# Turning normalized rows: 32x32 blocks on the DVE and a trip through memory in place of TensorE transposes

## The chip, the core and the metric

The kernel runs on one core of a Trainium2 chip. The metric is device time in microseconds (us) of one execution. The engines are TensorE (PE, with its weight loads as PEld), VectorE (DVE), ScalarE (ACT), GpSimd (POOL) and SyncE (SP). SP does no arithmetic here: it issues DMAs. POOL issues DMAs too, those that convert or accumulate.

## The reference

Two layers of masked attention over 16 batches of 1024 tokens with 256 features, in float32. Layer 0 has four heads of 64, layer 1 eight heads of 32.

```python
# for each of two layers (weights and number of heads differ; layer 1 has biases for q, k and v)
h = jnp.maximum(_layernorm(x, axis=-1), 0.0)          # normalized rows, then relu
q, k, v = h @ Wq, h @ Wk, h @ Wv                      # split into heads
scores = q @ k.T / sqrt(D)
scores = where(adj > 0, scores, -inf)                 # adj: 1024 x 1024 a batch
out = softmax(scores, axis=-1) @ v
x = x + concat(heads of out) @ Wo.T + bo
```

x is (16, 1024, 256), adj is (16, 1024, 1024) of int32, about 3% ones.

## The kernel before

**Layout.** A batch is worked in two halves of 512 tokens. The rows of x of one half lie in a tile [128, 4, 256]: token 128 t + p is at partition p, slot t. Scores are computed transposed, keys on partitions and 512 queries along the row, so q and k are needed as [features, tokens]. That is what the turn is for: the normalized rows `hn` (tokens on partitions) become `hT` (features on partitions).

**Inputs of a half.** `stats` (DVE statistics, then four small POOL instructions), `norm` (four ACT instructions into `hn`, one buffer), `add_bias` (a POOL DMA that adds bo to x), `turn` (eight PE transposes into a PSUM pair, L209, and one ACT copy to `hT`, L210, two buffers), then `k`, `q` and `values`, matrix products from `hT` of about 3.7 us of PE each.

**Steps.** A layer's attention is cut into groups (a half of the queries times half of the heads), and a group into steps. Layer 0 has 16 steps a batch, layer 1 has 32. In a step PE computes four score blocks (L400) into two PSUM pairs; for each pair DVE applies the mask (L416) and ACT the exponential (L422); two steps later PE multiplies the result p by v (L434). The score blocks share three PSUM pairs with every other product. The sums of p for the softmax are formed by adding tiles of p: on DVE and POOL (L443 to L449) in layer 0; in layer 1 on POOL (L535) and by DMAs that add one tile of p into another (`accumulate`, L521, 1 MB each). PE then adds over partitions (L301, `pz`).

**End of a group.** `copy_out` (ACT, L312) brings the product to `cat`. `spread` copies the sums from PSUM to `s` (ACT, L320) and spreads them by DMA over the partitions (L333); `invert` takes the reciprocal (DVE, L341), writes it to memory as `vd` (L343) and reads it back over the partitions of each head as `inv` (L346); `normalize` multiplies on POOL (L352). After two groups `end_half` multiplies by Wo (L381), adds to x (L386) and, after layer 1, stores it.

**Masks.** For each of eight tiles of a batch's adj: `load` (POOL DMA with conversion to bf16 into `adj`, one buffer, L131), `flip` (SP's DMA transpose into `adjT`, one buffer, L137), `put` (ACT, L146, into the mask as fp8), and later `second` (ACT, L154).

**Order.** The order is written out by hand. `stream.later(i, f, ...)` puts function f into step i; within a step, small work comes first, then `turn` and the products. Each engine and each DMA-issuing queue runs its instructions in the order in which they were recorded, and a wait holds back all that stands behind it on the same queue. The batch loop interleaves layer 0 of batch b+1 (steps `a` to `a + 15`) with layer 1 of batch b (steps `c` to `c + 31`); `mine` is layer 1 of batch b, `other` is layer 0 of batch b+2. One pass of this loop is 48 steps. The lines that place the turns of a pass after the first, `half_inputs(inp, half, turn, k, q, values)`:

```python
half_inputs(mine, 0, a - 13, a, a + 2, a + 8)        # a - 13 is c + 19 of the pass before
half_inputs(mine, 1, a - 1, c, c + 6, c + 2)         # a - 1 is c + 31 of the pass before
half_inputs(other, 0, c + 1, c + 8, c + 16, c + 18)
half_inputs(other, 1, c + 9, c + 22, c + 26, c + 30)
```

Of the kernel before, what the change touches and what calls it, by code (L numbers as in the profile page):

```python
# [10 lines left out]
F32 = mybir.dt.float32  # L11
# [3 lines left out]
AF = mybir.ActivationFunctionType  # L15
# [3 lines left out]
P = 128  # L19
# [66 lines left out]
def fast_program(ctx, tc, a, w, loads, chk):  # L86
# [3 lines left out]
    nc = tc.nc  # L90
    x, adj, out = a["x"], a["adj"], a["out"]
    B, N, E = x.shape
# [5 lines left out]
    actp = ctx.enter_context(tc.tile_pool(name="actp", bufs=2))  # L98
# [14 lines left out]

    xs = {}

    def open_x(b, half):
        t = xp.tile([P, 4, E], F32, tag=f"x{half}", name=f"x_{b}_{half}")
        nc.sync.dma_start(t, x[b, ts(half, 512), :].rearrange("(t p) e -> p t e", p=P))
        xs[b, half] = t


# [35 lines left out]
    class Inputs:  # L157
# [25 lines left out]
                self.shift[half] = small.tile([P, 4], F32, tag="shift", bufs=3, name=f"shift_{n}")  # L183
                nc.gpsimd.tensor_mul(self.shift[half], less, self.rstd[half])

        def norm(self, half, tiles=range(4)):
            n = f"{self.n}_{half}"
            if 0 in tiles:
                self.hn[half] = work.tile([P, 4, E], F32, tag="hn", bufs=1, name=f"hn_{n}")
            for i in tiles:  # L190
                nc.scalar.activation(
                    self.hn[half][:, i, :], xs[self.b, half][:, i, :], AF.Relu,
                    bias=self.shift[half][:, i : i + 1], scale=self.rstd[half][:, i : i + 1],
                )

        def add_bias(self, half):
# [3 lines left out]
                rows, w.bo[self.layer].unsqueeze(1).to_broadcast([P, 4, E]), accum_op=ALU.add  # L200
            )

        def turn(self, half):
            hn = self.hn.pop(half)
            self.hT[half] = actp.tile([P, 2, 512], F32, tag="hT", name=f"hT_{self.n}_{half}")
            pt = psum_pair(f"ph_{self.n}_{half}")
            for c in range(2):
                for i in range(4):
                    nc.tensor.transpose(pt[:, c, ts(i, P)], hn[:, i, ts(c, P)], w.ident)  # L209
            nc.scalar.copy(self.hT[half], pt)  # L210

        def kq(self, half, is_q):
            if half == 0 and not is_q:
# [58 lines left out]
    class Group:  # L272
# [36 lines left out]
        def copy_out(self):  # L309
            if self.g == 0:  # L310
                self.half.cat = work.tile([P, 2, 512], F32, tag="cat", name=f"cat_{self.n}")
            nc.scalar.copy(self.half.cat[:, self.g, :], self.o)  # L312

        def lanes(self, t):
            return t.rearrange("r (c f) -> (r c) f", f=self.n_f)
# [1 line left out]
        def spread(self):  # L317

            s = work.tile([P, 512], F32, tag="s", bufs=1, name=f"s_{self.n}")
            nc.scalar.copy(s, self.s)  # L320
            inp, k = self.inp, 2 * self.qh + self.g
            if k == 0:

                pool, tag = small, f"sums{self.layer}"
                if self.layer and inp.b == B - 1:
                    pool, tag = adjp, "adj"
                inp.sums = pool.tile(
                    [P, 4 * self.n_f], F32, tag=tag, bufs=1, name=f"sums_{inp.n}"
                )
            self.sn = inp.sums[:, ts(k, self.n_f)]  # L330
            lanes = P // self.per
            for r in range(self.per):
                nc.sync.dma_start(  # L333
                    self.sn[r * lanes : (r + 1) * lanes, :],
                    s[r * self.D : r * self.D + 1, :].rearrange("r (c f) -> r c f", f=self.n_f),
                )
# [17 lines left out]
        def finish(self):  # L354

            inp, qh = self.inp, self.qh
            inv = work.tile([P, 512], F32, tag="inv", bufs=1, name=f"inv_{self.n}")
            py = psum_pair(f"py_{self.n}").rearrange("p a (t e) -> p (a t) e", e=E)
            rows, cat = xs[inp.b, qh], self.half.cat
            dst = out[inp.b, ts(qh, 512), :].rearrange("(t p) e -> p t e", p=P)  # L360
            for h in range(2):
                q = ts(h, 256)
                nc.vector.reciprocal(inv[:, q], self.s[:, q])
                nc.vector.tensor_mul(cat[:, self.g, q], cat[:, self.g, q], inv[:, q])
                for i in (2 * h, 2 * h + 1):
                    for c in range(2):
                        nc.tensor.matmul(
                            py[:, i, :], cat[:, c, ts(i, P)], w.o[self.layer][:, c, :],
                            start=(c == 0), stop=(c == 1),
                        )  # L370
            for h in range(2):
                t = ts(h, 2)
                nc.vector.tensor_add(rows[:, t, :], py[:, t, :], rows[:, t, :])
                nc.sync.dma_start(dst[:, t, :], rows[:, t, :])

        def end_half(self):
            inp, qh = self.inp, self.qh
            py = psum_pair(f"py_{self.n}").rearrange("p a (t e) -> p (a t) e", e=E)
            for i in range(4):
                for c in range(2):  # L380
                    nc.tensor.matmul(  # L381
                        py[:, i, :], self.half.cat[:, c, ts(i, P)], w.o[self.layer][:, c, :],
                        start=(c == 0), stop=(c == 1),
                    )
            rows = xs[inp.b, qh]
            nc.vector.tensor_add(rows, py, rows)  # L386
            if self.layer:
                nc.sync.dma_start(
                    out[inp.b, ts(qh, 512), :].rearrange("(t p) e -> p t e", p=P), rows
                )  # L390

    def scores(st):
        gr = st.gr
# [66 lines left out]
    class Stream:  # L460
# [12 lines left out]
        def later(self, i, f, *args):  # L473
            self.due.setdefault(i, []).append((f, args))
# [116 lines left out]
    mask, inp = masks[0], inputs[0][0]  # L591
# [11 lines left out]
    inp.stats(0)  # L603
    load(0)
    load(1)
    inp.norm(0)
    inp.stats(1)
    load(2)
    load(3)
# [7 lines left out]
    flip(1)  # L617
    open_w(1)
    inp.k(0)
    inp.norm(1)  # L620
    for u in range(4, NT):
        load(u)
    inp.q(0)
# [41 lines left out]
    stream = Stream(steps)  # L665
    later = stream.later

    def norms(inp, half, *at):

        for i, f in zip(at, (inp.stats, inp.stats, inp.norm, inp.norm)):  # L670
            later(i, f, half, (0, 1) if i in (at[0], at[2]) else (2, 3))
        later(at[3] + 1, inp.add_bias, half)

    def half_inputs(inp, half, *at):

        for i, f in zip(at, (inp.turn, inp.k, inp.q, inp.values)):
            later(i, f, half)


# [6 lines left out]
        later(i - 2, masks[1].flip, t)  # L686
        later(i, masks[1].put, t)
    later(9, bias_of_v)
    norms(inputs[0][1], 0, 2, 3, 5, 6)
    half_inputs(inputs[0][1], 0, 7, 8, 10, 12)  # L690
    norms(inputs[0][1], 1, 6, 7, 9, 10)
    half_inputs(inputs[0][1], 1, 13, 14, 20, 16)
    for b in range(B - 1):
        mine, a, c = inputs[1][b], first[b + 1], second[b]
        if b == 0:

            norms(mine, 0, a + 5, a + 6, a + 8, a + 9)
            half_inputs(mine, 0, a + 11, a + 12, a + 14, a + 14)
            norms(mine, 1, a + 13, a + 14, a + 15, c)
            half_inputs(mine, 1, c + 1, c + 3, c + 6, c + 4)  # L700
        else:
            norms(mine, 0, a - 20, a - 19, a - 16, a - 15)
            half_inputs(mine, 0, a - 13, a, a + 2, a + 8)
            norms(mine, 1, a - 14, a - 10, a - 8, a - 6)
            half_inputs(mine, 1, a - 1, c, c + 6, c + 2)
        for i, u in zip((0, 2, 4, 6, 8, 10, 12, 13), range(NT)):
            later(a + i, masks[b].second, u)
        if b + 2 < B:
            other, mask = inputs[0][b + 2], masks[b + 2]
            later(a + 5, open_x, b + 2, 0)  # L710
            later(a + 13, open_x, b + 2, 1)
            if b == 0:
                norms(other, 0, a + 14, a + 15, c + 2, c + 3)
                half_inputs(other, 0, c + 5, c + 8, c + 16, c + 18)
                norms(other, 1, c + 3, c + 4, c + 6, c + 7)
                half_inputs(other, 1, c + 11, c + 22, c + 26, c + 30)
            else:
                norms(other, 0, a + 10, a + 12, a + 13, a + 15)
                half_inputs(other, 0, c + 1, c + 8, c + 16, c + 18)
                norms(other, 1, c, c + 4, c + 5, c + 6)  # L720
                half_inputs(other, 1, c + 9, c + 22, c + 26, c + 30)
            for i, t in zip((7, 12, 17, 22, 33, 37, 41, 45), range(NT)):
                later(a + i - 6, mask.load, t)
                later(a + i - 3, mask.flip, t)
                later(a + i, mask.put, t)
        else:
            last, e = inputs[1][b + 1], c + 32
            norms(last, 0, c + 5, c + 6, c + 8, c + 9)
            half_inputs(last, 0, c + 11, c + 14, c + 16, c + 20)
            norms(last, 1, c + 13, c + 14, c + 16, c + 17)  # L730
            half_inputs(last, 1, c + 19, c + 24, e + 6, e + 4)
            for u in range(NT):
                later(c + 8 + 2 * u, masks[b + 1].second, u)
    stream.run()
# [249 lines left out]
```

## Time and profile before

| | |
|---|---|
| median of 3 runs | 3334.15 us (3329.18 to 3335.32) |
| the profiled execution's own time | 3336.89 us |
| its span, first to last instruction | 3335.1 us |
| mean granted TensorE clock | 0.991 |
| one pass of the batch loop, from the accumulates that recur in the chain | about 205 us |
| the turn: 512 transposes (L209), 64 copies (L210) | 72.0 us of PE, 64.2 us of ACT |
| PE waiting for `hT`, before values, k or Wo | 16.2 + 2.5 + 1.9 us |
| POOL's mask load waiting for a flip | 76.4 us, 29 times |
| DMA, moved | 361.08 MB, mean 108 GB/s |

The page gives, for each engine, the time in which it was busy and its share of the span; busy PE time has modelled ends. The chain of work that ended last is followed back from the last instruction, at each step to what released it; what stands in it set the end. A timeline lists one engine's instructions by start, with its idle time before them and who ended it. In the view by stretches the figures after the engines are the clock, the busy share of the 16 DMA engines and GB/s.

### The profile page before, as it was taken

How to read it: one execution, taken by the hardware profiler on the slowest of the kernel's cores; microseconds unless marked ns; L12 is line 12 of the kernel's file. 1: busy time of each engine (PE TensorE's matmuls, PEld its weight loads, DVE VectorE, ACT ScalarE, POOL GpSimd, SP SyncE). 2: the span in 40 equal slices, each digit the busy share in tenths (PEclk: the TensorE clock that was granted, in tenths of full speed). 3: DMA queues.
4: the chain of work that ended last, by engine and by line, in shares of the span. 5: the costliest groups of instructions: out<-in, count | busy, mean ns of one | idle time of the engine just before them, and what ended most of it. 6: DMA issues, size and time to landing. Idle time of an engine off the chain costs nothing.

```text
span 3335.1 us, 44057 instructions
## 1 busy us (share of the span) xinstructions
PE 3245.4 (97%) x16766; PEld 1272.1 (38%) x16766; DVE 2391.8 (72%) x2600; ACT 2308.4 (69%) x2530; POOL 2349.9 (70%) x1274
## 2 busy tenths in 40 slices
PE   8999999999999999999999999999999999999998
PEld 3443333433434343343434334333333433333333
DVE  5677776777767677676777767767677776776766
ACT  5667676776767767677676766767767676676765
POOL 4568576785867858677686766867768576685776
PEclk9999999999999999999999999999999999999999
DMA  7338467384663836548375583755737557383441
GB/s 147 66 66 150 93 111 140 75 154 87 123 125 80 160 82 130 112 94 148 79 141 101 99 140 77 136 106 106 135 80 146 105 105 138 71 146 78 85 85 31
DMA packets 313485, 361.08 MB, mean 108 GB/s; under 512 B 190001, under 2 KB 257841, under 8 KB 290481
## 3 DMA queue, kind: packets, MB, share of 16 engines
q0 software_dynamic: 77856, 253.78, 42.3%
q1 hardware_dynamic: 235408, 104.41, 13.9%
q8 instruction: 133, 2.18, 0.3%
q14 instruction: 88, 0.71, 0.1%
HBM read 119.54 MB, written 17.56 MB: 41 GB/s over the span
## 4 chain that ended last, share of the span: by engine, by line
PE 72%; POOL 8%; DMA 8%; DVE 4%; ACT 4%; issue 3%; SPq 1%; POOLq 0%; DVEq 0%; ACTq 0%
PE ps L400 24%; PE po L434 21%; PE pq L226 11%; PE pv L262 6%; POOL p L535 5%; PE py L381 5%; DMA p<-p 4%; PE pz L301 3%; DVE p L416 3%; DMA adjT<-adj 2%; ACT p L422 2%; PE ph L209 1%; POOL p L446 1%; ACT mask L146 1%; DMA vd<-vn 1%
## 5 line engine op out<-in xcount | busy, mean ns | idle before, releaser
L416 DVE SCALAR_TENSOR_TENSOR p<-mask,ps 128x1024 f32<-128x1024 fp8e5 x1536 | 1793.8, 1215 | 698.8 <-PE ps L400 606.5
L422 ACT ACTIVATE p<-p 128x1024 f32<-128x1024 f32 x1536 | 1614.5, 1057 | 820.5 <-DVE p L416 776.1
L535 POOL TENSOR_TENSOR p<-p,p 128x2048 f32<-128x2048 f32 x255 | 1202.5, 4718 | 171.0 <-PE po L434 157.7
L400 PE MATMUL ps<-qT,kT 32*128 32x512 f32 (+1 forms) x6144 | 1194.0, 638 | 25.6 <-DVE p L416 23.9
L434 PE MATMUL po<-p,v 128*32 128x512 f32 (+1 forms) x6144 | 998.1, 606 | 1.8 <-ACT cat L312 1.8
L400 PEld LDWEIGHTS ps<-qT,kT 32*128 32x128 f32 (+1 forms) x6144 | 383.0, 185 | 724.8 <-issue 374.5
L447 POOL TENSOR_TENSOR p<-p 128x1024 f32<-128x1024 f32 x128 | 301.8, 2358 | 298.3 <-DVE p L446 293.2
L434 PEld LDWEIGHTS po<-p,v 128*32 128x32 f32 (+1 forms) x6144 | 229.2, 118 | 696.6 <-issue 509.8
L446 POOL TENSOR_TENSOR p<-p 128x1024 f32<-128x1024 f32 x64 | 151.5, 2367 | 253.8 <-DVE p L443 169.4
L262 PE MATMUL pv<-wv,hT 128*128 128x256 f32 x1024 | 237.8, 385 | 16.2 <-ACT hT L210 16.2
L521 POOL DMA_DIRECT2D p<-p x178 | 178.5, 1003 | 95.1 <-DMA p<-p 66.6
L226 PE MATMUL pq<-hT,wq 128*128 128x512 f32 x512 | 242.4, 617 | 0.1
L226 PE MATMUL pq<-hT,wk 128*128 128x512 f32 x512 | 238.9, 610 | 2.7 <-ACT hT L210 2.5
L381 PE MATMUL py<-wo,cat 128*128 128x256 f32 x1008 | 233.9, 385 | 3.1 <-ACT hT L210 1.9
L262 PEld LDWEIGHTS pv<-wv,hT 128*128 128x128 f32 x1024 | 189.4, 190 | 88.5 <-ACT hT L210 27.7
L381 PEld LDWEIGHTS py<-wo,cat 128*128 128x128 f32 x1008 | 186.5, 190 | 72.8 <-issue 46.4
L352 POOL TENSOR_TENSOR cat<-cat,inv 128x512 f32<-128x512 f32 x127 | 173.9, 1369 | 9.8 <-DMA inv<-vd 8.6
L301 PE MATMUL pz<-p,ones 128*32 128x512 f32 (+1 forms) x888 | 148.7, 595 | 16.2 <-DMA p<-p 15.4
L443 DVE TENSOR_TENSOR p<-p 128x1024 f32<-128x1024 f32 x128 | 156.3, 1221 | 0.0
L449 POOL TENSOR_TENSOR p<-p,p 128x1024 f32<-128x1024 f32 x64 | 151.7, 2370 | 5.0
L312 ACT COPY cat<-po 128x512 f32<-128x512 f32 x128 | 74.0, 578 | 115.9 <-PE po L434 115.9
L226 PEld LDWEIGHTS pq<-hT,wq 128*128 128x128 f32 x512 | 94.3, 194 | 146.2 <-issue 119.9
(50 smaller groups left out, 1754.6 us busy)
## 6 DMA issues: line engine op xcount, KB each, us to landing
p<-p POOLq DMA_DIRECT2D x178, 1024.0 KB, 8.7
adj<-in_adj_dram POOLq DMA_DIRECT2D x128, 256.0 KB, 4.2
x<-bo POOLq DMA_DIRECT2D x64, 512.0 KB, 6.0
x<-in_x_dram SPq DMA_DIRECT2D x32, 512.0 KB, 3.9
inv<-vd SPq DMA_DIRECT2D x128, 128.0 KB, 2.9
inv<-vd SPq DMA_DIRECT2D x252, 64.0 KB, 4.8
out_dram<-x SPq DMA_DIRECT2D x31, 512.0 KB, 4.5
sums<-s SPq DMA_DIRECT2D x384, 2.0 KB, 2.8
```

Source lines behind the costliest of these rows:

```text
L226: nc.tensor.matmul(pq[:, m, :], wt[self.layer][:, c, ts(m, P)], self.hT[half][:, c, :], start=(c == 0), stop=(c == 1),)
L262: nc.tensor.matmul(pv[:, i, :], self.hT[half][:, c, ts(i, P)], w.v[self.layer][:, c, :], start=(c == 0), stop=(c == 1),)
L301: nc.tensor.matmul(self.s[r * self.D : (r + 1) * self.D, :], w.ones.to_broadcast([P, self.D]), p[:, r, :], start=start, stop=stop,)
L381: nc.tensor.matmul(py[:, i, :], self.half.cat[:, c, ts(i, P)], w.o[self.layer][:, c, :], start=(c == 0), stop=(c == 1),)
L400: nc.tensor.matmul(st.ps[i // 2][:, i % 2, :], gr.inp.kT[r * D : (r + 1) * D, gr.g, ts(kt, P)], gr.inp.qT[gr.qh][r * D : (r + 1) * D, gr.g ...
L416: nc.vector.scalar_tensor_tensor(out=half, in0=gr.mask.m[gr.qh][:, kt, :].unsqueeze(1).to_broadcast([P, 2, 512]), scalar=-EDGE if gr.layer ...
L422: nc.scalar.activation(half, half, AF.Exp, scale=gr.scale)
L434: nc.tensor.matmul(gr.o[r * D : (r + 1) * D, :], gr.inp.v[:, kt, h * D : (h + 1) * D], st.p[:, i, :], start=(kt == 0), stop=(kt == NT - 1),)
L446: engine.tensor_add(b, two.p[:, 0:2, :], two.p[:, 2:4, :])
L447: nc.gpsimd.tensor_add(a, a, b)
L521: nc.gpsimd.dma_start(one, two, accum_op=ALU.add)
L535: nc.gpsimd.tensor_add(one, one, st.p)
```

## The change

Token p of a half is laid out anew. The half is cut into four groups of 128 tokens; token 128 g + 32 t + p sits at partition 32 g + p, slot t. So x is loaded, and the result stored, in four DMAs of 32 partitions each instead of one of 128.

In 58 of the 64 turns `norm` writes `hn` in blocks, for each 32 features the four slots beside each other. One DVE instruction transposes every 32x32 block of `hn` in place (`turn_blocks`). Within each partition group that gives 128 consecutive tokens for a feature. `put_blocks` writes the 512 KB tile to memory as `turned`, and `place_blocks` reads it back in four DMAs into `hT`, whose contents are as before. Six early turns (`whole=True` in their norms) stay on TensorE. Where columns are tokens and rows of x are to come out (`cat`, `s`, `inv`), the copies permute the columns in runs of 32.

```diff
+    def quarters(of, b, half):
+        rows = of[b, ts(half, 512), :].rearrange("(g t p) e -> g p t e", g=4, p=32)
+        return [rows[g] for g in range(4)]
+    def by_tile(cols):
+        return cols.rearrange("p (g t q) -> p t g q", g=4, q=32)
+    def tiled(cols):
+        return cols.rearrange("p (t g q) -> p t g q", g=4, q=32)
...
-        nc.sync.dma_start(t, x[b, ts(half, 512), :].rearrange("(t p) e -> p t e", p=P))
+        for g, rows in enumerate(quarters(x, b, half)):
+            nc.sync.dma_start(t[ts(g, 32)], rows)
...
-                    self.hn[half][:, i, :], xs[self.b, half][:, i, :], AF.Relu,
+                    hn[:, ts(i, E)] if whole else self.blocks(half)[:, :, i, :],
+                    rows if whole else rows.rearrange("p (c q) -> p c q", q=32), AF.Relu,
...
+        def blocks(self, half):
+            return self.hn[half].rearrange("p (c t q) -> p c t q", t=4, q=32)
...
-                    nc.tensor.transpose(pt[:, c, ts(i, P)], hn[:, i, ts(c, P)], w.ident)
+                    nc.tensor.transpose(by_tile(pt[:, c, :])[:, i], hn[:, i, ts(c, P)], w.ident)
...
+        def turn_blocks(self, half):
+            nc.vector.transpose(self.hn[half], self.hn[half])
+        def put_blocks(self, half):
+            n = f"{self.n}_{half}"
+            self.turned = dram.tile([P, 4 * E], F32, tag="turned", bufs=2, name=f"turned_{n}")
+            nc.sync.dma_start(self.turned, self.hn.pop(half))
+        def place_blocks(self, half):
+            hT = actp.tile([P, 2, 512], F32, tag="hT", name=f"hT_{self.n}_{half}")
+            self.hT[half] = hT
+            blocks = self.turned.rearrange("(g p) (c k q) -> k p c g q", p=32, k=4, q=P)
+            for k in range(4):
+                nc.sync.dma_start(
+                    hT[ts(k, 32)].rearrange("p c (g q) -> p c g q", q=P), blocks[k]
+                )
...
-            nc.scalar.copy(self.half.cat[:, self.g, :], self.o)
+            nc.scalar.copy(tiled(self.half.cat[:, self.g, :]), by_tile(self.o))
...
-            nc.scalar.copy(s, self.s)
+            nc.scalar.copy(tiled(s), by_tile(self.s))
...
-                nc.sync.dma_start(
-                    out[inp.b, ts(qh, 512), :].rearrange("(t p) e -> p t e", p=P), rows
-                )
+                for g, to in enumerate(quarters(out, inp.b, qh)):
+                    nc.sync.dma_start(to, rows[ts(g, 32)])
...
+    def block_inputs(inp, half, turn, place, *at):
+        later(turn, inp.turn_blocks, half)
+        later(place, inp.put_blocks, half)
+        later(place + 1, inp.place_blocks, half)
+        for i, f in zip(at, (inp.k, inp.q, inp.values)):
+            later(i, f, half)
...
-            half_inputs(mine, 0, a - 13, a, a + 2, a + 8)
+            block_inputs(mine, 0, a - 14, a - 12, a, a + 2, a + 8)
...
-            half_inputs(mine, 1, a - 1, c, c + 6, c + 2)
+            block_inputs(mine, 1, a, a + 6, c, c + 6, c + 2)
...
-                half_inputs(other, 0, c + 1, c + 8, c + 16, c + 18)
+                block_inputs(other, 0, c, c + 1, c + 8, c + 16, c + 18)
...
-                half_inputs(other, 1, c + 9, c + 22, c + 26, c + 30)
+                block_inputs(other, 1, c + 7, c + 8, c + 22, c + 26, c + 30)
```

In a pass the block transposes thus stand in steps c (other, half 0), c + 7 (other, half 1), c + 18 (mine, half 0) and a (mine, half 1); the writes to memory in c + 1, c + 8, c + 20 and a + 6; the reads one step after each of these. The products k, q and values keep their steps, and so do the statistics, the norms and the masks. The last batch of layer 1 has its two transposes in its steps c + 10 and c + 18.

More of the change, by code (lines that the diff above doesn't have):

```diff
@@ L184, in stats, with norm @@
                 nc.gpsimd.tensor_mul(self.shift[half], less, self.rstd[half])
-        def norm(self, half, tiles=range(4)):
+        def norm(self, half, tiles=range(4), whole=False):
             n = f"{self.n}_{half}"
             if 0 in tiles:
-                self.hn[half] = work.tile([P, 4, E], F32, tag="hn", bufs=1, name=f"hn_{n}")
+                self.hn[half] = work.tile([P, 4 * E], F32, tag="hn", bufs=1, name=f"hn_{n}")
+            hn = self.hn[half]
             for i in tiles:
+                rows = xs[self.b, half][:, i, :]
                 nc.scalar.activation(
-                    self.hn[half][:, i, :], xs[self.b, half][:, i, :], AF.Relu,
+                    hn[:, ts(i, E)] if whole else self.blocks(half)[:, :, i, :],
+                    rows if whole else rows.rearrange("p (c q) -> p c q", q=32), AF.Relu,
                     bias=self.shift[half][:, i : i + 1], scale=self.rstd[half][:, i : i + 1],
@@ L201, in add_bias @@
             )
+        def blocks(self, half):
+            return self.hn[half].rearrange("p (c t q) -> p c t q", t=4, q=32)
         def turn(self, half):
-            hn = self.hn.pop(half)
+            hn = self.hn.pop(half).rearrange("p (t e) -> p t e", e=E)
             self.hT[half] = actp.tile([P, 2, 512], F32, tag="hT", name=f"hT_{self.n}_{half}")
@@ L359, in finish @@
             rows, cat = xs[inp.b, qh], self.half.cat
-            dst = out[inp.b, ts(qh, 512), :].rearrange("(t p) e -> p t e", p=P)
+            dst = quarters(out, inp.b, qh)
             for h in range(2):
                 q = ts(h, 256)
-                nc.vector.reciprocal(inv[:, q], self.s[:, q])
+                nc.vector.reciprocal(tiled(inv)[:, ts(h, 2)], by_tile(self.s)[:, ts(h, 2)])
                 nc.vector.tensor_mul(cat[:, self.g, q], cat[:, self.g, q], inv[:, q])
@@ L373, in finish @@
                 nc.vector.tensor_add(rows[:, t, :], py[:, t, :], rows[:, t, :])
-                nc.sync.dma_start(dst[:, t, :], rows[:, t, :])
+                for g in range(4):
+                    nc.sync.dma_start(dst[g][:, t, :], rows[ts(g, 32), t, :])
         def end_half(self):
@@ L605, in fast_program @@
     load(1)
-    inp.norm(0)
+    inp.norm(0, whole=True)
     inp.stats(1)
@@ L619, in fast_program @@
     inp.k(0)
-    inp.norm(1)
+    inp.norm(1, whole=True)
     for u in range(4, NT):
@@ L666, in fast_program, with norms @@
     later = stream.later
-    def norms(inp, half, *at):
+    def norms(inp, half, *at, whole=False):
         for i, f in zip(at, (inp.stats, inp.stats, inp.norm, inp.norm)):
-            later(i, f, half, (0, 1) if i in (at[0], at[2]) else (2, 3))
+            rest = (whole,) if i in at[2:] else ()
+            later(i, f, half, (0, 1) if i in (at[0], at[2]) else (2, 3), *rest)
         later(at[3] + 1, inp.add_bias, half)
@@ L688, in fast_program @@
     later(9, bias_of_v)
-    norms(inputs[0][1], 0, 2, 3, 5, 6)
+    norms(inputs[0][1], 0, 2, 3, 5, 6, whole=True)
     half_inputs(inputs[0][1], 0, 7, 8, 10, 12)
-    norms(inputs[0][1], 1, 6, 7, 9, 10)
+    norms(inputs[0][1], 1, 6, 7, 9, 10, whole=True)
     half_inputs(inputs[0][1], 1, 13, 14, 20, 16)
@@ L695, in fast_program @@
         if b == 0:
-            norms(mine, 0, a + 5, a + 6, a + 8, a + 9)
+            norms(mine, 0, a + 5, a + 6, a + 8, a + 9, whole=True)
             half_inputs(mine, 0, a + 11, a + 12, a + 14, a + 14)
-            norms(mine, 1, a + 13, a + 14, a + 15, c)
+            norms(mine, 1, a + 13, a + 14, a + 15, c, whole=True)
             half_inputs(mine, 1, c + 1, c + 3, c + 6, c + 4)
@@ L713, in fast_program @@
                 norms(other, 0, a + 14, a + 15, c + 2, c + 3)
-                half_inputs(other, 0, c + 5, c + 8, c + 16, c + 18)
+                block_inputs(other, 0, c + 4, c + 5, c + 8, c + 16, c + 18)
                 norms(other, 1, c + 3, c + 4, c + 6, c + 7)
-                half_inputs(other, 1, c + 11, c + 22, c + 26, c + 30)
+                block_inputs(other, 1, c + 10, c + 11, c + 22, c + 26, c + 30)
             else:
                 norms(other, 0, a + 10, a + 12, a + 13, a + 15)
-                half_inputs(other, 0, c + 1, c + 8, c + 16, c + 18)
+                block_inputs(other, 0, c, c + 1, c + 8, c + 16, c + 18)
                 norms(other, 1, c, c + 4, c + 5, c + 6)
-                half_inputs(other, 1, c + 9, c + 22, c + 26, c + 30)
+                block_inputs(other, 1, c + 7, c + 8, c + 22, c + 26, c + 30)
             for i, t in zip((7, 12, 17, 22, 33, 37, 41, 45), range(NT)):
@@ L728, in fast_program @@
             norms(last, 0, c + 5, c + 6, c + 8, c + 9)
-            half_inputs(last, 0, c + 11, c + 14, c + 16, c + 20)
+            block_inputs(last, 0, c + 10, c + 11, c + 14, c + 16, c + 20)
             norms(last, 1, c + 13, c + 14, c + 16, c + 17)
-            half_inputs(last, 1, c + 19, c + 24, e + 6, e + 4)
+            block_inputs(last, 1, c + 18, c + 19, c + 24, e + 6, e + 4)
             for u in range(NT):
```

## The prediction

> **What bounds the kernel now.** I read the page's busy shares first, then the chain of work that ended last, then that chain over one pass of the batch loop (1177 to 1382 us), then the timelines of SP, POOL, ACT and DVE beside it. The page:
>
> ```profile
> PE 3245.4 (97%) x16766; PEld 1272.1 (38%) x16766; DVE 2391.8 (72%) x2600; ACT 2308.4 (69%) x2530; POOL 2349.9 (70%) x1274
> ...
> PE 72%; POOL 8%; DMA 8%; DVE 4%; ACT 4%; issue 3%; SPq 1%; POOLq 0%; DVEq 0%; ACTq 0%
> ```
>
> PE is the bound for most of the time, not for all of it: 28% of the chain lies elsewhere. A pass takes 205 us, and I count its steps as a+0 to a+15 (layer 0 of batch b+1) and c+0 to c+31 (layer 1 of batch b). The chain of that pass, pieces that bear on the change:
>
> ```profile
> 1245.62 0.92 ACT hT L210
> ...
> 1277.14 1.02 PE ph L209 x8
> ...
> 1312.18 1.02 PE ph L209 x8
> ...
> 1330.46 3.25 DMA adjT<-adj
> ...
> 1335.86 4.59 POOL p L535
> ...
> 1340.47 1.23 DVE p L416
> ...
> 1355.75 1.02 PE ph L209 x8
> ```
>
> Columns: start, length, what. Three of the pass's four turns (c+9, c+19, c+31) stand in the chain with their 1.02 us of PE; the one at c+1 is there through the copy of hT, for which PE then waited (1.11 us idle before pv in the same place one pass earlier). But from 1330 to 1342 (c+24 to c+28) PE does not set the time. A mask flip, the DMA adjT<-adj, does. SP's timeline shows why the flip came so late:
>
> ```profile
> 1308.51 3.98 SPq L333 DMA_DIRECT2D sums<-s  x4
> 1312.59 1.86 SPq L137 DMA_TRANSPOSE adjT<-adj  x1
> 1319.12 0.35 SPq L343 DMA_DIRECT2D vd<-vn  x1
> 1327.27 3.03 SPq L346 DMA_DIRECT2D inv<-vd  x4
> 1330.46 1.26 SPq L137 DMA_TRANSPOSE adjT<-adj  x1
> ```
>
> SP issues in order. It sat from 1319.5 to 1327.3 on the landing of vd, 8 KB, before it could issue inv, and the flip stood behind that. Who waits for the flip, from the timelines of POOL and ACT:
>
> ```profile
> 1334.28 0.66 POOL L131 DMA_DIRECT2D adj<-in_adj_dram  x1 [3.59 <-DMA adjT<-adj]
> ```
> ```profile
> 1334.37 1.14 ACT L146 ACTIVATE mask<-adjT,numbers 128x1024 fp8e5<-128x1024 bf16 x1
> ```
>
> adj has one buffer, so POOL's next mask load waits for the flip's landing (1333.71), and with it the add L535 that frees p for DVE at c+27. ACT's L146 reads the flip's result at 1334.37, only 0.66 us after it landed, and the exponentials of c+26 are behind it. A later flip is therefore a later c+27, nearly one for one. And the DMA engines are fullest just here. The view of busy time by stretches gives, after each engine's busy time, the clock, the DMA share (0.91) and GB/s:
>
> ```profile
> 1303.00:1330.00 27.00, 27.00 (x180) 10.44 (x176) 20.26 (x25) 22.93 (x25) 23.74 (x13) 1.00 0.91 165
> ```
>
> **What the Trainium skill says.** "VectorE: DVE Perf Modes", The three transpose paths: the DVE turns 32x32 blocks only and can't span banks, hence the trip through memory. "DMA: Bandwidth & Descriptors", Two DMAs through the same engine are not ordered: a DMA that reads what another wrote has to wait for its semaphore before it is issued; the trace shows such a wait as SP's 7.8 us above. Same page, Queues, rings and completion order: each engine takes queues in turn, packet by packet. That agrees with vd's 8.1 us beside POOL's 1 MB accumulates (its median is 1.5 us in the issues table). "SBUF — State Buffer", Who interferes with whom: a DVE instruction with one SBUF input outside the two-port modes doesn't contend with GpSimd; no transpose is in this trace to check it.
>
> **The change part by part.** 58 of 64 turns go the new way: four a pass, 14 times each, and two at the end. Six (three early sets of two) stay on TensorE.
>
> *PE, removed.* A turn is 8 transposes that hold PE for 1.03 us (1277.14 to 1278.17 in the chain). At c+1: 1.03 + 1.11 of waiting = 2.14, times 14 = 30.0 us. At c+9 and c+31: 1.03 x 28 = 28.8. At the end 2 x 1.03 = 2.1. At c+19: 14.4, but that one lies between SP's sums and the late flip, where SP and the DMAs set the time; I credit it with nothing here and with 14.4 in the fast case. Removed: 60.9 us, or 75.3.
>
> *ACT.* 58 copies of 1.00 us go; ACT isn't the bound, so nothing. The norms now write runs of 32 floats, and 256 copies (L312, L320) read PSUM in such runs: nothing, since L146, which writes runs of 128 bytes, takes 1135 ns where the contiguous L154 takes 1133. Bounds 0 to 0.1 us each.
>
> *DVE, added.* 58 block transposes of 1024 elements. No row of the trace has one. The page on the DVE gives (N+151)/0.96 ns for an fp32 add at one element a cycle (The TRN2 errata), 1224 for 1024 elements, and L443 takes 1221 here; I take 1.22 us as an estimate for the transpose too, bounds 1.1 (L416 back to back, 1.14) and 2.3 (half that rate). They stand at c+0, c+7, c+18 and a+0. In the pass before, DVE idled 1.19 us after the statistics at c+0 and 1.21 at c+18; at a+0 it has 3.4 us until the next L416. At c+7 only 0.3 is free, but c+8 is followed by 1.5 idle while PE runs pq. Nothing on the path; if the cover is gone, 71 us.
>
> *SP and the DMAs, added.* Each turn issues one put of 512 KB (it waits for the transpose) and four places of 128 KB (they wait for the put to land). x is loaded and out stored in four pieces each, 0.46 us an issue. Waits of ACT for hn and of SP for a free hT: hn is next written 4 or more steps after the put (one step in the first pass), hT's last reader is 3 or more steps before the places; nothing. At c+2 and c+9 the places have 6 and 13 steps until k, and no flip within 3 us: nothing. At a+7 vd and inv get some 4 us later; the product L352 of a+10 started at 1415.4 one pass later, inv was issued by 1407.5 and lands in some 3: nothing, with a us to spare.
>
> At c+20/c+21 it is different. SP's order there becomes flip (c+18), put, places, vd, inv, flip (c+22). Worked out on the times above: put issued 1314.5 behind the flip; a 512 KB load takes 3.9 us to land, so 1319 to 1322 with the accumulate issued at 1317.5 beside it. Four issues at 0.8: 1322 to 1325.5. vd follows instead of at 1319.1, and lies in SP's rings behind 512 KB of pieces of 512 bytes, which themselves share the engines with two accumulates until about 1330: it lands at 1331 to 1334 instead of 1327.2. inv 3 us, flip at 1334 to 1338 instead of 1330.5. So the flip is 3.5 to 8 us later, taken 6.5; times 14 = 91 us.
>
> *Start and end.* First x in four issues: 3 x 0.49 = 1.5 us before DVE's first statistics. Last store: 3 x 0.46 = 1.4.
>
> *Sum.* -60.9 + 91 + 2.9 = +33 us on the profiled execution's own 3336.9 us (span 3335.1), which lies 2.7 above the median of the runs, 3334.2. On the median: 3367.
>
> **Rivals.** *The hole is big enough* (faster): the put goes through between 1314.5 and 1318, where the accumulate has hardly begun, and the places before vd; the flip is late by 1 us at most. Then -75.3 + 14 + 2.9 = -58: 3276. For it: DMA is busy 0.55 before 1303, and SP has long idle stretches; against it: 0.91 just there. The two cases part where the flip's delay is what a pass gains without c+19, 58.8/14 = 4.2 us. *DVE pays what PE saved* (no change): the transposes are not covered, 71 us back: -75.3 + 71 + 2.9 = -1, 3333. Against it, the idle times above. *All DMAs get slower* (slower still): 61 MB more on 361 MB, 17%, stretches the accumulates that pz and p wait for; a flip delay of 11 us: -60.9 + 154 + 2.9 = +96, 3430. *It doesn't do what it says*: runs of 32 floats cost the copies double, 256 x 0.57 = 146 us of ACT; L146 speaks against it, and ACT has slack; under 5%.
>
> **How the numbers follow.** A measurement of this kernel tells 0.2%, some 7 us, from no change. Late flip: 0.50 (3340 to 3400 by its own bounds, 3.5 to 8 us and 1 us of other cost a pass). Everything slower: 0.10. Fast: 0.33, own range 3262 to 3315. In between or DVE pays: 0.07. Cases of both signs hold most of the chance, so the range takes in the fast case to its centre and the slow one nearly to its own: 3274 to 3418. Faster 0.33, same 0.07, slower 0.60.
>
> **What would show it.** Right: SP's timeline at c+20 to c+22 with the places waiting for turned and vd issued 3 us or more later; POOL's L131 waiting over 7 us for adjT<-adj in each pass, over 150 us in all instead of 76.4; DVE at c+27 that much later; from c+0 to c+17 a pass shorter by 3 us. Wrong: L131's wait unchanged, or DVE's L416 waiting for less of PE with the transposes right before late scores.

## The result and the profile after

The changed kernel takes 3356.17 us (median of 15 runs, 3338.4 to 3371.24) where the kernel before takes 3334.15: a ratio of 1.006, 95% interval 1.0042 to 1.0078, so 22 us slower. The profiled execution took 3353.67 us (span 3351.9 us, mean granted TensorE clock 0.981), 16.8 above the one of before.

The page of the changed kernel, busy times and the shares of the chain of work that ended last:

```profile
PE 3228.7 (96%) x16302; PEld 1230.2 (37%) x16302; DVE 2459.4 (73%) x2658; ACT 2256.7 (67%) x2472; POOL 2349.5 (70%) x1274
...
PE 68%; POOL 11%; DMA 9%; DVE 4%; issue 3%; ACT 2%; SPq 2%; POOLq 0%; DVEq 0%; ACTq 0%
```

464 of PE's instructions are gone and DVE has 58 more, as the change says. PE lost 4 points of the chain, and POOL gained 3, SP's queue and the DMAs 1 each. What grew is in the waits of the changed kernel (who waited <- for whom: us in all, times, longest). Before, the first three were 86.8, 76.4 and 2.5:

```profile
DVE p L453 <- POOL p L572: 152.3, 92, 8.3
POOL adj L145 <- DMA adjT<-adj: 129.4, 31, 9.6
ACT mask L160 <- DMA adjT<-adj: 34.3, 16, 5.3
```

(L145 is L131 of before, L160 is L146, L453 is L416, L572 is L535.) Flips are waited for longer, by POOL and now by ACT too, and DVE waits longer for POOL. SP's timeline in the same pass, around c+18 to c+22:

```profile
1312.68 3.88 SPq L370 DMA_DIRECT2D sums<-s  x4
1316.67 1.94 SPq L151 DMA_TRANSPOSE adjT<-adj  x1
1318.71 0.76 SPq L238 DMA_DIRECT2D turned<-hn  x1
1321.89 4.07 SPq L245 DMA_DIRECT2D hT<-turned  x4
1326.06 1.25 SPq L380 DMA_DIRECT2D vd<-vn  x1
1333.76 2.01 SPq L383 DMA_DIRECT2D inv<-vd  x4
1335.88 1.30 SPq L151 DMA_TRANSPOSE adjT<-adj  x1
```

The order is the predicted one: flip, put, places (3.2 us after the put, for its landing), vd, inv, flip. vd took 7.7 us from its issue to the issue of inv; in the pass that the prediction read it had taken 8.1 with no put or places ahead of it. It landed right behind the places: the last of them at 1333.5, vd at 1333.7. The places themselves took long in this stretch (in ns the min, median and max of an issue, in us the times from issue to landing):

```profile
L245 SPq DMA_DIRECT2D hT<-turned x4: 607/974/1367, 1321.9 to 1324.6; - x4
DMA to landing us min/median/max: 8.9/9.4/9.5
```

Who pays, from POOL's timeline:

```profile
1341.01 0.66 POOL L145 DMA_DIRECT2D adj<-in_adj_dram  x1 [5.98 <-DMA adjT<-adj]
1341.66 0.93 POOL L558 DMA_DIRECT2D p<-p  x1
1342.25 4.90 POOL L572 TENSOR_TENSOR p<-p,p 128x2048 f32<-128x2048 f32 x1
1346.77 1.61 POOL L389 TENSOR_TENSOR cat<-cat,inv 128x512 f32<-128x512 f32 x1
1347.99 4.88 POOL L572 TENSOR_TENSOR p<-p,p 128x2048 f32<-128x2048 f32 x1
```

and from DVE's:

```profile
1347.19 4.62 DVE L453 SCALAR_TENSOR_TENSOR p<-mask,ps 128x1024 f32<-128x1024 fp8e5 x4 [3.06 <-POOL p L572]
1352.91 1.22 DVE L453 SCALAR_TENSOR_TENSOR p<-mask,ps 128x1024 f32<-128x1024 fp8e5 x1 [1.10 <-POOL p L572]
```

POOL stands 5.98 us before the mask load, and two adds of 4.9 us stand behind it on the same engine. DVE waits for the first (3.06 us) and for the second (1.10).

To see where a pass gains and loses, I took PE's first score product of each step from the trace; the table has the mean us from step to step over twelve passes. The columns after the first two are experiments, told below.

| steps | before | after | e1 | e2 | e3 | e5 | e8 |
|---|---|---|---|---|---|---|---|
| a to c | 81.04 | 81.24 | 81.09 | 81.28 | 81.05 | 81.07 | 81.24 |
| c to c+10 | 45.00 | 41.77 | 41.77 | 41.77 | 45.01 | 41.77 | 41.77 |
| c+10 to c+14 | 12.52 | 13.04 | 13.03 | 13.04 | 12.48 | 13.04 | 13.04 |
| c+14 to c+18 | 13.95 | 13.89 | 13.89 | 13.89 | 13.89 | 13.89 | 13.89 |
| c+18 to c+24 | 21.07 | 21.44 | 21.14 | 22.88 | 20.54 | 21.53 | 21.09 |
| c+24 to c+28 | 15.35 | 16.40 | 15.90 | 15.72 | 15.57 | 15.88 | 15.30 |
| c+28 to c+30 | 7.39 | 10.05 | 6.47 | 8.22 | 9.71 | 6.87 | 6.62 |
| c+30 to a | 9.47 | 8.13 | 8.74 | 8.65 | 9.54 | 8.62 | 8.84 |

The change gains 3.23 us by c+10, gives 0.52 back by c+14, and from c+18 to c+30, where it took one more turn off PE, it is 4.08 longer.

### The profile page after: what moved, and what is told of

The parts are those of the page before. It is cut to its first block, busy times and chain, and to the rows that moved or that the text cites. A ratio compares the mean times of both kernels' runs of the same rounds, so it can differ in the third digit from the quotient of the medians.

```text
span 3351.9 us, 43993 instructions
## 1 busy us (share of the span) xinstructions
PE 3228.7 (96%) x16302; PEld 1230.2 (37%) x16302; DVE 2459.4 (73%) x2658; ACT 2256.7 (67%) x2472; POOL 2349.5 (70%) x1274
## 4 chain that ended last, share of the span: by engine, by line
PE 68%; POOL 11%; DMA 9%; DVE 4%; issue 3%; ACT 2%; SPq 2%; POOLq 0%; DVEq 0%; ACTq 0%
PE ps L437 24%; PE po L471 20%; PE pq L263 10%; POOL p L572 8%; PE pv L299 6%; PE py L419 5%; DMA adjT<-adj 3%; DMA p<-p 3%; PE pz L338 3%; DVE p L453 3%; DMA vd<-vn 1%; SPq L370 1%; POOL p L483 1%; ACT p L459 1%; POOL p L558 1%
## 5 line engine op out<-in xcount | busy, mean ns | idle before, releaser
L453 DVE SCALAR_TENSOR_TENSOR p<-mask,ps 128x1024 f32<-128x1024 fp8e5 x1536 | 1794.4, 1215 | 635.5 <-PE ps L437 477.3
L572 POOL TENSOR_TENSOR p<-p,p 128x2048 f32<-128x2048 f32 x255 | 1204.6, 4726 | 135.4 <-PE po L471 124.4
L437 PE MATMUL ps<-qT,kT 32*128 32x512 f32 (+1 forms) x6144 | 1220.5, 642 | 63.2 <-DVE p L453 58.8
L263 PE MATMUL pq<-hT,wq 128*128 128x512 f32 x512 | 250.4, 634 | 0.1
L145 POOL DMA_DIRECT2D adj<-in_adj_dram x128 | 87.8, 688 | 133.9 <-DMA adjT<-adj 129.4
L338 PE MATMUL pz<-p,ones 128*32 128x512 f32 (+1 forms) x888 | 148.7, 596 | 17.6 <-DMA p<-p 16.8
L160 ACT ACTIVATE mask<-adjT,numbers 128x1024 fp8e5<-128x1024 bf16 x124 | 140.8, 1136 | 34.3 <-DMA adjT<-adj 34.3
```

The source lines that it names most:

```text
L263: nc.tensor.matmul(pq[:, m, :], wt[self.layer][:, c, ts(m, P)], self.hT[half][:, c, :], start=(c == 0), stop=(c == 1),)
L338: nc.tensor.matmul(self.s[r * self.D : (r + 1) * self.D, :], w.ones.to_broadcast([P, self.D]), p[:, r, :], start=start, stop=stop,)
L437: nc.tensor.matmul(st.ps[i // 2][:, i % 2, :], gr.inp.kT[r * D : (r + 1) * D, gr.g, ts(kt, P)], gr.inp.qT[gr.qh][r * D : (r + 1) * D, gr.g ...
L453: nc.vector.scalar_tensor_tensor(out=half, in0=gr.mask.m[gr.qh][:, kt, :].unsqueeze(1).to_broadcast([P, 2, 512]), scalar=-EDGE if gr.layer ...
L572: nc.gpsimd.tensor_add(one, one, st.p)
```

## The experiments

Two theories. **Order**: mine's half 0 puts its DMAs into SP's queue between the flips of c+18 and c+22, and the flip comes late. **Load**: the block turns cost by what they add anywhere, DVE time, DMA traffic, the new layout. All were timed in five rounds beside the kernel before.

**e1: mine's half 0 back on TensorE, the other three by blocks.**

```diff
-            norms(mine, 0, a - 20, a - 19, a - 16, a - 15)
-            block_inputs(mine, 0, a - 14, a - 12, a, a + 2, a + 8)
+            norms(mine, 0, a - 20, a - 19, a - 16, a - 15, whole=True)
+            half_inputs(mine, 0, a - 13, a, a + 2, a + 8)
```

> As after, but the turn of layer 1's half 0 (c+18 to c+21) goes back to TensorE at c+19; the other 44 turns stay with the DVE and memory. Late flip in SP's queue: that place held all of the loss, so what is left is the gain of the other places, some 47 to 61 us: 3275 to 3295 us. More DMA traffic, wherever it stands: a quarter of the traffic goes, so a quarter of loss and gain: about 3345. DVE pays what PE saved: about 3350, as only 14 of 58 transposes go.

Measured: 3295.65 us, ratio 0.9877 (0.9848 to 0.9906). One turn of four carries the whole loss and more: with it back on TensorE the change gains 38 us. The waits of e1 are near those of before again (the flip 76.4 then, POOL's add 86.8):

```profile
DVE p L453 <- POOL p L572: 102.0, 81, 3.1
POOL adj L145 <- DMA adjT<-adj: 82.9, 30, 4.3
```

**e2: mine's half 0 by blocks, places two steps later, at c+23, behind vd, inv and the flip of c+22.**

```diff
-            block_inputs(mine, 0, a - 14, a - 12, a, a + 2, a + 8)
+            later(a - 14, mine.turn_blocks, 0)
+            later(a - 12, mine.put_blocks, 0)
+            later(a - 9, mine.place_blocks, 0)
+            for i, f in zip((a, a + 2, a + 8), (mine.k, mine.q, mine.values)):
+                later(i, f, 0)
```

> As after, but layer 1's half 0 is read back in step c+23 instead of c+21, so that SP issues vd, inv and the flip of c+22 ahead of the four reads; every transfer stays, in nearly the same stretch. Late flip in SP's queue: the flip is as early as before, POOL's load waits some 3.5 us in each pass again, 3265 to 3295 us. More DMA traffic: nothing gained, 3345 to 3365. DVE pays: 3350 to 3360.

Measured: 3319.35 us, ratio 0.9952 (0.9932 to 0.9971). That is 37 us less than the changed kernel, only by where four DMAs stand in a queue, but 24 short of e1: order is the larger part, not all. In its profile one pass of 226.8 us (c+18 to c+21 in 35.9) stands beside others of 201 to 208 and one of 213.9; the mean in the table contains it.

**e3: mine's half 0 alone by blocks, as in the changed kernel; the others on TensorE.**

```diff
-            block_inputs(mine, 1, a, a + 6, c, c + 6, c + 2)
+            half_inputs(mine, 1, a - 1, c, c + 6, c + 2)
...
-                block_inputs(other, 0, c, c + 1, c + 8, c + 16, c + 18)
+                half_inputs(other, 0, c + 1, c + 8, c + 16, c + 18)
...
-                block_inputs(other, 1, c + 7, c + 8, c + 22, c + 26, c + 30)
+                half_inputs(other, 1, c + 9, c + 22, c + 26, c + 30)
```

> The other way about: only layer 1's half 0 is turned by the DVE and memory (14 turns), all others by TensorE in the new layout. Late flip in SP's queue: the loss alone, slower than before by 45 to 85 us, 3380 to 3420. More DMA traffic: a quarter of the whole change's effect, 3335 to 3345. DVE pays: no change, 3335 to 3340.

Measured: 3371.6 us, ratio 1.0115 (1.0087 to 1.0143). Alone it costs 34 us against e4, less than forecast, and less than the 60 us by which the changed kernel lies above e1: beside the other three the same turn costs more, and no run shows why. In the table it takes 0.53 off c+18 to c+24 and adds 2.32 at c+28 to c+30.

**e4: no turn by blocks, only the new layout** (every `block_inputs` a `half_inputs`).

> All 64 turns on TensorE; only the new layout of the tokens is left: x and the result in four DMAs each, ACT's copies and the transposes' output in runs of 32. Late flip: start and end alone, plus 3 us, 3332 to 3342. Copies in runs of 32 cost ACT time: most of the 22 us or more, 3350 and up, with L349 and L357 over 600 ns instead of 575.

Measured: 3337.96 us, ratio 1.0013 (1.0002 to 1.0023). The layout costs some 4 us (by the interval 0.7 to 7.7), and no more. Its copies with runs of 32 take 579 ns (L349) where the contiguous ones before took 578.

**e5: places of mine's half 0 at c+27, behind every flip of the pass.**

```diff
-            later(a - 9, mine.place_blocks, 0)
+            later(a - 5, mine.place_blocks, 0)
```

> As the changed kernel, but mine's half 0 is placed at c+27, behind every flip of the pass; its put stays at c+20, ahead of vd. Order (the places stood ahead of the flip of c+26 when they were at c+23, and the flip then waits): the rest of the loss goes, 3280 to 3300, no later than the kernel whose half 0 turns on TensorE (3295.7). Traffic (a megabyte through memory beside the accumulates, or the put ahead of vd): it stays where the placing at c+23 left it, 3310 to 3325.

Measured: 3307.44 us, ratio 0.9934 (0.9913 to 0.9956). Another 12 us, between the two forecasts; so the later the places, the less they cost: 3356 at c+21, 3319 at c+23, 3307 at c+27. But it doesn't reach e1.

**e6: e1 with the put alone.** The normalized rows of mine's half 0 are written to memory at c+19, and nobody reads them.

```diff
+            later(a - 13, mine.put_unread, 0)
             half_inputs(mine, 0, a - 13, a, a + 2, a + 8)
```

> As the kernel whose mine's half 0 turns on TensorE (3295.7), with one thing more: the normalized rows of that half are also put to memory at c+19 (512 KB in each pass, one DMA on SP's queue), where nothing reads them. If the put alone, its bytes and its place ahead of vd, carries what is left: 3310 to 3325. If only the places count, or the flips they stand ahead of: 3293 to 3302.

Measured: 3291.17 us, ratio 0.9873 (0.9852 to 0.9893), no more than e1. 512 KB more in the fullest stretch of the DMAs, ahead of vd, cost nothing that shows here. What costs is on the side of the places, or on what happens to the turn itself.

**e7: e1 with every block transpose made three times.**

```diff
-            nc.vector.transpose(self.hn[half], self.hn[half])
+            for _ in range(3):
+                nc.vector.transpose(self.hn[half], self.hn[half])
```

> As the kernel whose mine's half 0 turns on TensorE (3295.7), with each of its 44 block transposes on the DVE made three times (three give what one gives), so 88 x 1.24 = 109 us more of DVE. If the DVE's time at these places is covered (the prediction's step): 3296 to 3310. If the DVE pays: up to 3400; if only the place at c+7 is uncovered, as 0.55 us given back at c+10 to c+14 suggests, 14 x 2.5 = 35 us, about 3330.

Measured: 3370.48 us, ratio 1.0112 (1.0091 to 1.0133): 75 us of the 109 added reached the end. Step by step, the stretch c to c+10 takes 3.0 us more than in e1, of which 0.5 come at c+3, behind the transposes at c, and 2.5 at c+8 and c+9, behind those at c+7; c+10 to c+14 takes 0.9 more, a to c 0.1. So at c+7 two more transposes don't fit at all, at c they fit but for half a microsecond, and at a they fit. This is a price of more, not of the first one, which e8 asks for.

**e8: e1 with other's half 1 transposed one step later.**

```diff
-                block_inputs(other, 1, c + 7, c + 8, c + 22, c + 26, c + 30)
+                block_inputs(other, 1, c + 8, c + 9, c + 22, c + 26, c + 30)
```

> As the kernel whose mine's half 0 turns on TensorE (3295.7), with other's half 1 transposed on the DVE one step later, at c+8 (put c+9, places c+10), where the DVE is done 1.6 us ahead of the next scores. If the transpose at c+7 holds the DVE's masks back (0.5 us a pass at c+10 to c+14): 14 x 0.5 = 7 us less, 3285 to 3291. If those 0.5 us have another cause (the layout, the traffic of put and places at c+8 and c+9): 3293 to 3300.

Measured: 3289.68 us, ratio 0.9872 (0.9855 to 0.9888). The total is where the first theory put it, but the stage is not: c+10 to c+14 stays at 13.04. So the transpose at c+7 was covered, as predicted, and the half microsecond has another cause. It shows in DVE's timeline of e8 in that stretch:

```profile
1269.84 2.35 DVE L453 SCALAR_TENSOR_TENSOR p<-mask,ps 128x1024 f32<-128x1024 fp8e5 x2 [0.50 <-PE ps L437]
1272.66 4.61 DVE L453 SCALAR_TENSOR_TENSOR p<-mask,ps 128x1024 f32<-128x1024 fp8e5 x4 [0.47 <-POOL p L572]
```

and in POOL's:

```profile
1268.06 4.57 POOL L572 TENSOR_TENSOR p<-p,p 128x2048 f32<-128x2048 f32 x1 [0.92 <-PE po L471]
```

At c+11 DVE waits for POOL to finish this add; before, with PE a turn later, the same six masks ran on from 1279.27 without a stop.

**e9: e8 with mine's half 0 by blocks as well, transposed at c+17, put at c+19, placed at c+27.**

```diff
-            norms(mine, 0, a - 20, a - 19, a - 16, a - 15, whole=True)
-            half_inputs(mine, 0, a - 13, a, a + 2, a + 8)
+            norms(mine, 0, a - 20, a - 19, a - 17, a - 16)
+            later(a - 15, mine.turn_blocks, 0)
+            later(a - 13, mine.put_blocks, 0)
+            later(a - 5, mine.place_blocks, 0)
+            for i, f in zip((a, a + 2, a + 8), (mine.k, mine.q, mine.values)):
+                later(i, f, 0)
```

> As the kernel with other's half 1 at c+8, and mine's half 0 by blocks too, one step earlier (norms at c+15 and c+16, transpose at c+17, put at c+19) and placed at c+27. If what its turn gives (1.03 us at c+18 to c+21) was only eaten by its transpose at c+18 (0.6 at c+21 to c+24): 14 x 1.0 less than that kernel, 3272 to 3282. If its places beside the accumulates cost what they did in the kernel placed at c+27: 3290 to 3305.

Measured: 3306.94 us, ratio 0.9942 (0.9922 to 0.9962), as e5. The turn gives nothing in this place even with its places behind every flip: c+18 to c+24 is 0.35 shorter than in e8, c+24 to c+28, where the places now stand, is 1.89 longer.

**e10: e8 less one of POOL's adds a pass**, the one that DVE waits for at c+11. The sums of that group lack a part; its time is read for this stretch alone.

```diff
-                nc.gpsimd.tensor_add(one, one, st.p)
+                if not (j == 7 and gr.qh == 0 and gr.g == 0):
+                    nc.gpsimd.tensor_add(one, one, st.p)
```

> As the kernel with other's half 1 at c+8 (3289.7), without one of POOL's adds (4.57 us) a pass: that of the eighth step of layer 1's first group, made at c+9; the denominators of that group lack one part, so the output is not the reference's. If that add is what now holds DVE's masks at c+11 (0.47 us of waiting there) and so eats half of what the turn at c+9 gave: c+10 to c+14 goes from 13.04 back to about 12.5, 14 x 0.5 = 7 us less, 3279 to 3285. If something else paces that stretch: 3287 to 3293.

Measured: 3282.08 us, ratio 0.9841 (0.9828 to 0.9855), 7.6 less than e8, and c+10 to c+14 takes 12.48. Both are the forecast of the first theory. What the turn at c+9 freed on PE, POOL took back by half.

**e11 and e12: the flips of c+18 and c+22 at c+17 and c+20**, their mask loads at c+14 and c+17, ACT's `put` of these masks at c+20 and c+23. Both flips then stand ahead of vd. The second load now stands in the same step as the flip that it has to wait for, c+17; before it stood one step after it. e11 is e8 so changed, e12 the changed kernel.

```diff
-            for i, t in zip((7, 12, 17, 22, 33, 37, 41, 45), range(NT)):
+            for i, t in zip((7, 12, 17, 22, 33, 36, 39, 45), range(NT)):
```

> As the kernel with other's half 1 at c+8 (3289.7), with the flips of c+18 and c+22 at c+17 and c+20 (mask loads at c+14 and c+17), so that both stand ahead of vd in SP's queue. If the flip behind vd sets the time from c+24 to c+28 (the prediction's reading of the kernel before): 1 to 3 us a pass less, 3245 to 3278. If POOL's adds set it anyway: 3284 to 3294. If the mask loads and flips beside the accumulates only move the stall: up to 3310.

> The changed kernel (3356.2), all turns by blocks, with the same two flips at c+17 and c+20, so that put and places of mine's half 0 stand behind the flip of c+20 and still ahead of vd. If the late flip carries the loss: it falls to within 15 us of the kernel that has these flips and mine's half 0 on TensorE. If the places and vd carry it by the late inv, or by their traffic: 3325 to 3360.

Measured: e11 3303.56 us, ratio 0.9907 (0.9892 to 0.9922), and e12 3418.62, ratio 1.0258 (1.0234 to 1.0281). In e11 the third of the cases came true, the stall moves; in e12 both missed. In e11 the stretch c+24 to c+30 falls from 21.92 to 17.50; but c+18 to c+24 rises from 21.09 to 26.96. POOL's timeline of e11 shows the new place of the stall:

```profile
1306.66 0.59 POOL L145 DMA_DIRECT2D adj<-in_adj_dram  x1 [3.63 <-DMA adjT<-adj]
1307.70 1.32 POOL L216 DMA_DIRECT2D x<-bo  x1 [0.45 <-ACT p L459]
1308.50 5.09 POOL L572 TENSOR_TENSOR p<-p,p 128x2048 f32<-128x2048 f32 x1
```

The mask load, earlier now, waits 3.63 us for the flip before it, again with an add behind it. In e12 the places still stand ahead of vd; the flip that stood behind them now stands ahead, and inv is late. SP's timeline of e12:

```profile
1340.80 0.90 SPq L238 DMA_DIRECT2D turned<-hn  x1
1349.39 4.49 SPq L245 DMA_DIRECT2D hT<-turned  x4
1353.98 0.88 SPq L380 DMA_DIRECT2D vd<-vn  x1
1359.29 4.13 SPq L383 DMA_DIRECT2D inv<-vd  x4
```

and POOL's:

```profile
1366.91 1.27 POOL L389 TENSOR_TENSOR cat<-cat,inv 128x512 f32<-128x512 f32 x1 [4.50 <-DMA inv<-vd]
1368.14 4.52 POOL L572 TENSOR_TENSOR p<-p,p 128x2048 f32<-128x2048 f32 x1
```

Here SP stood 7.7 us until the put had landed (1341.7 to 1349.4), inv came late, and POOL waited for inv with an add behind it. So POOL waits in this stretch for the flips and for inv, which all come from SP's one queue; whichever is late, POOL's adds are late.

## Why the prediction was right, and where it was off

It said slower, by what the order on SP's queue at c+20 and c+21 does, at 3367 us; the place is shown by e1 and e3, the kind by e2 and e5. That the sum fell on the right side is in part luck. Of its 33 us, 32 were to come from the passes, 2.3 in each; in the profiled execution a pass is longer by 0.17 us on the mean of twelve, and 10.5 us of the loss lie at the start, in the first 64 steps and at the end (the last point below). By its steps:

- **PE removed.** For c+1 and c+9 it had 3.17 us a pass; c to c+10 got shorter by 3.23. For c+31 it had 1.03, and that step alone is 1.02 shorter. It took both as lasting. But 0.52 of it is given back at c+10 to c+14, behind POOL's add (e10), 7 us in all: what is taken off the bound counts only as far as the next engine keeps up.
- **DVE, covered.** The transpose takes 1239 ns where 1.22 us was estimated:

```profile
L233 DVE STREAM_TRANSPOSE hn<-hn x58: 1237/1239/1247, 227.0 to 3179.2; 128x1024 f32<-128x1024 f32 x58
```

  (a view by tile: min, median, max in ns, first and last start.) e8 shows the one at c+7 covered, and a to c, within 0.2 us of before, the one at a; e7 shows how little cover is left. The rival in which DVE takes back what PE saved was wrong for one transpose in each place; with three (e7) it comes true.
- **ACT and layout.** Nothing for ACT and 2.9 us for start and end; e4 has some 4 for all of it.
- **The flip's delay, 6.5 us.** This is the mis-sized term. The stretch that it was charged to, c+18 to c+30, got 4.08 us longer, 57 us in 14 passes where 91 were forecast. Where the delay went, in us from c+18's first score, mean of the twelve passes:

| | before | after |
|---|---|---|
| vd issued | 14.65 | 19.39 |
| inv issued, vd having landed | 20.35 | 27.50 |
| flip of c+22 issued | 24.05 | 29.75 |
| this flip landed | 29.78 | 33.72 |
| POOL's mask load behind it starts | 30.53 | 34.28 |

  The queue did to the flip about what was forecast: it is issued 5.7 us later. But it lands only 3.9 later (by the medians 3.2 and 2.7). The prediction had read one pass, and took the landing to follow the issue. Before, vd landed within 4 us in four of the twelve passes and the flip was issued early, at 19 to 22; it landed at 26 to 34 all the same. In the other eight it was issued at 25 to 27 and landed at 28 to 30.

  In the pass shown the put landed in 3.1 us where 4.5 to 7.5 were taken, so the places went out sooner than forecast. vd landed right behind them, in each of the twelve passes 0.16 to 0.20 us after the last one, and its own time went from 5.7 to 8.1 us on the mean, but how much of that is due to the places isn't shown: before, without them, it took 1.5 to 8.9. What the prediction took from "The Trainium skill", "DMA: Bandwidth & Descriptors", Queues, rings and completion order, is that an engine takes its queues in turn, packet by packet; that doesn't say how long vd waits behind the pieces of its own queue, and no run here varies this alone.
- **"Nearly one for one".** Off the other way. From c+18 to c+30 a pass takes 4.08 us more although 1.03 of PE went there, so 5.1 were paid for a load that starts 3.8 later. In the pass shown the delay passes through two POOL adds of 4.9 us, and DVE waits for both. Over the kernel DVE's waits for POOL grew by 65.5 us, and ACT's wait for the flips went from 2.5 to 34.3. PE's clock can be up to 1.7 of the 5.1 (last section); no run separates these. The two errors cancel in part: 4.08 against the 6.5 forecast, and close to the 4.2 that the prediction named as break-even. So the passes are almost even (205.79 us before, 205.96 after, the sums of the table's columns).
- **Its signs.** The places stand ahead of vd, vd is issued 4.7 us later, and c to c+18 is 2.8 us shorter where 3 were forecast. POOL's wait for the flips came to 129.4 us, short of the 150 named.
- **The rest.** Of the 16.8 us between the profiled executions, the start gives 1.0, the first 64 steps 4.3, the following thirteen passes 6.3 (4.4 of them in the last one), the remainder 5.2. The prediction had 2.9 for start and end. The 4.3 is a wait that it put at nothing: it counted 6 steps from the places of other's half 0 to k, but in the first pass these places stand in c+6 and k in c+8. PE's timeline of that step:

```profile
248.37 5.37 PE L263 MATMUL pq<-hT,wk 128*128 128x512 f32 x8 [3.94 <-DMA hT<-turned]
```

  PE waits 3.94 us for hT, and the product then takes 5.37 us where it took 3.70 before, with the clock at half from 248.7 on. c to c+10 of this pass is 4.6 us longer than before, 4.9 in e1, whose other halves stand in the same places, and unchanged in e3 and e4, where this turn is on TensorE. Of the remaining 5.2 us e4 has 2.8 and e1 0.3; the end stays unexplained.

Open: why mine's half 0 by blocks, placed at c+27, still costs 12 to 17 us against TensorE (e5 against e1, e9 against e8). The put by itself is ruled out (e6), the step of the transpose makes no difference (e9), and the flip of c+22 isn't late: it lands 30.9 us after c+18's first score in e5, 30.6 in e1. Left are the places' traffic late in the pass, POOL taking back PE's microsecond as at c+11, and PE's clock. In e9 DVE waits 2.5 us a pass for POOL from c+18 to c+24, in e8 0.9; and PE has half speed for 5.1 us a pass in e9, for 2.3 in e8. No run here parts the three. Open too: single passes near 2.1 ms that are 4 to 25 us longer, in before, after, e2, e5, e9 and e12, at different size each time.

The best kernel here whose sums are whole is e8: three of four turns by blocks, mine's half 0 on TensorE, 3289.68 us, ratio 0.9872 to before. e1 differs from it by no more than its runs spread.

## What to carry to other kernels

Work moved off the bound engine to a DMA can cost nothing by its bytes (the put of e6) and more than it gains by the place it takes in an in-order queue: list what stands behind each new issue and who waits for that, and then what stands behind the waiter on its own engine. Try each moved piece by itself and beside the others; here three of four were worth 38 us and the fourth took 60 (34 alone). Read a wait over several passes before pricing it (vd took 1.5 to 8.9 us in the passes before), and count the steps of the first pass apart. A gain on the bound lasts only as far as the next engine's slack, so look for the second bound's long instructions (here POOL's adds of 4.6 to 4.9 us) right behind the place where time is saved.

## What the hardware showed that was not expected

The trip of 512 KB through memory looks quick by its medians. The issues table of the changed kernel (KB each, median us from issue to landing) has

```profile
p<-p POOLq DMA_DIRECT2D x178, 1024.0 KB, 9.5
...
turned<-hn SPq DMA_DIRECT2D x58, 512.0 KB, 3.5
hT<-turned SPq DMA_DIRECT2D x232, 128.0 KB, 4.2
```

against 8.7 us for p<-p before: with 61 MB more the median of POOL's accumulates is 0.8 us longer. But in the stretch that counts, at c+20 and c+21 of the pass shown, where the DMA engines are busy 0.89 of the time, the put took 3.1 us and the places 8.9 to 9.5; in e12 the put took 8.5 in its place. The median of the 8 KB vd over the kernel went from 1.5 us to 3.4.

A stall can also leave PE slower for a while after it. "The Trainium skill", "TensorE: Matmul & The Clock Gate", Part 1: The HAM clock gate, says that after an idle window of about 3.4 us PE's clock is halved until it has been busy for about as long. The view by stretches of the pass shown, in the kernel after: first c+24 to c+28, then 3.4 us ahead of a halving in it and 3.4 us from there on (the first figure after the length is PE's busy time; the last three are the clock, the DMA share and GB/s):

```profile
1329.18:1345.72 16.54, 15.86 (x84) 4.89 (x80) 8.87 (x8) 11.78 (x15) 10.41 (x7) 0.90 0.89 166
1334.10:1337.50 3.40, 2.72 (x17) 0.63 (x9) 2.43 (x3) 1.86 (x4) 0.93 (x1) 1.00 0.98 222
1337.50:1340.90 3.40, 3.40 (x4) 1.49 (x5) 2.18 (x2) 1.74 (x3) 0.00 (x0) 0.50 0.81 110
```

(The clock was 1.00 from c+24 to c+28 before, and 0.78 from c+28 to c+30, where it is 1.00 after.) The length agrees with the page: within the passes the clock records show half speed for 3.41 us or two or three times that. The idle time doesn't: PE was idle for 0.7 us of the 3.4 ahead of this halving, and for 0.8 to 1.6 us ahead of those in the passes before (busy PE time has modelled ends). So far shorter stalls than the page's can be followed by half speed.

Summed over the trace's clock records, PE was granted half speed for 62 us before and 129 after, with 54 in e1, in line with the mean clocks, 0.991, 0.981 and 0.992. Half of the 67 us more, some 33, is what it can have cost at most. From c+18 to c+30 it is 3.7 us a pass before and 7.1 after, so at most 1.7 us of a pass; how much of it stood in the path no run separates. The prediction, which moved a stall, had no term for it.
